# Layer 1: four narrow low-rank products side by side, their factors fetched by number, and a written TensorE order

## The chip, the cores and the metric

The kernel runs on one core of one Trainium2 chip. The metric is the device time of one execution in microseconds (us). The kernel before was run three times: the median is 3809.74 us, the lowest 3806.65 and the highest 3811.78. One more execution was recorded by the hardware profiler.

Five engines work side by side: TensorE (PE, matrix products, with its weight loads shown apart as PEld), VectorE (DVE), ScalarE (ACT), GpSimd (POOL) and SyncE (SP, which here issues DMA transfers). The matrix products write to PSUM. Everything is in fp32.

## The reference

The network has three layers and a tail. 64 sequences of 32 tokens, 2048 tokens of width 512, pass through all of it. The change touches only layer 1, and of it mainly the first half, a gated feed-forward block with low-rank updates. Each sequence has a number (`itok_B_2_6`, between 2 and 6), and by it picks its own pair A, B of rank 16 for each of the three products:

```python
def lora_add(base, inp, A, B):
    Ab = A[layer_idx][lora_indices]
    Bb = B[layer_idx][lora_indices]
    t = jnp.einsum('bri,bni->bnr', Ab, inp)
    return base + jnp.einsum('bor,bnr->bno', Bb, t) * SCALE
gate = lora_add(jnp.einsum('bnh,fh->bnf', x, W_gate), x, A_gate, B_gate)
up = lora_add(jnp.einsum('bnh,fh->bnf', x, W_up), x, A_up, B_up)
act = jax.nn.silu(gate) * up
down = lora_add(jnp.einsum('bnf,hf->bnh', act, W_down), act, A_down, B_down)
```

The width of `gate`, `up` and `act` is 1376. There are 16 sets of A and B. What the document calls the **first half** of an update is `t`, the product with A; the second half is the product with B.

The second part of layer 1 is a mixture of eight rank-16 updates on top of one base product: every token gets weights over the eight from a softmax and a threshold, and the result is added to x.

## The kernel before

A tile holds 128 tokens, that is four sequences. Layer 1 (`layer1`, L249 to L381) runs over eight groups g of G=2 tiles, so N=256 tokens and eight sequences. Every product has its contraction in chunks of at most 128: KC=4 chunks for the width 512, and the eleven chunks FC (`NFC`) for the width 1376, the last of which has 96.

A tile framework follows reads and writes, puts in the semaphores, and its scheduler chooses the order on each engine by what is ready; in layer 1 of this kernel nothing fixes the order on TensorE. Buffers come from pools: a second tile of the same tag waits until the first one's readers are done. In PSUM layer 1 has the tags `tr`, `low`, `gate` and `up`, two buffers each[...].

In one group:

- `inputs` (L282) loads two tiles of x through SP (`load`, L85) and gathers, with an indirect DMA on POOL (`gather`, L278), the rows of A and B of the eight sequences: eight times rank 16 gives 128 rows. There are six gathers: Ag, Au, Ad, Bg, Bu, Bd.
- x is transposed on TensorE and copied by ACT (`transposed`, L117 and L118) to xT.
- For Ag and Au the same is done, which gives AT; then one product of all 128 rows of A with all 256 tokens runs over four chunks (`accumulate`, L122, tile `pt`). Of the 128x256 results only those in which the row's sequence is the token's are wanted: DVE multiplies with the mask `own` (L311), which also holds the factor 0.5.
- Ad is transposed in eleven pieces (L317, tile `pa`) and copied by ACT to AdT.
- For each of the eleven chunks of features, `pg` and `pu` take four products with the weights and one with Bg or Bu each; ACT computes the sigmoid (L333), DVE multiplies twice (L334, L335) and writes actT.
- AdT with actT gives the first half of down, eleven products, masked at L339. `pz` is down's product, with Bd as its last step, copied by ACT to zT (L346).
- For each tile the mixture follows: `ph` (logits and the eight first halves, 137 columns), a chain of small operations on DVE and ACT, `hw` (L389), its transpose, `po` (base product and second halves), the sum with x (L381), and the store through SP (L382).

The inputs of group g+1 are asked for behind down of group g. Before layer 1, `layer0` computes in groups of four tiles and stores its results to memory (L245), from where layer 1 reads them; its last steps for a tile use POOL at L126, L242 and L243 and wait for a load of x (L85). Layer 0's first product `py` (L183) is already made of narrow products: 32 columns of weights, each for one sequence, four side by side, 512 moving columns. Layer 2 (attention) follows layer 1 and starts with loads of its weights and products at L504 and L509.

A record pair, a weight load and a matmul, is one pass; a product in fp32 takes two of them, a transpose takes one.

Of the kernel before, what the change touches and what calls it, by code (L numbers as in the profile page):

```python
# [24 lines left out]
F32 = mybir.dt.float32  # L25
# [35 lines left out]
class Common:  # L61


    def __init__(self, ctx, tc, a):
        self.tc, self.nc, self.a = tc, tc.nc, a
        self.last_load = None
        self.last_pe = None
        pool = ctx.enter_context(tc.tile_pool(name="common", bufs=1))
        self.ident = pool.tile([P, P], F32, name="ident")
        make_identity(self.nc, self.ident)  # L70
        self.minus_half = pool.tile([P, 2 * HK], F32, name="minus_half")
        self.nc.gpsimd.memset(self.minus_half, -0.5)
# [176 lines left out]


def layer1(c, kp, x_in, x_out):
    tc, nc, a = c.tc, c.nc, c.a
    G = 2
    N = G * P
    NE, R = 8, 16
    NFC = len(FC)
    with ExitStack() as ctx:
        aps = [ctx.enter_context(tc.tile_pool(name=f"l1_gathered{i}", bufs=1)) for i in range(2)]
        xp = ctx.enter_context(tc.tile_pool(name="l1_x", bufs=4))
        gup = ctx.enter_context(tc.tile_pool(name="l1_gate_up", bufs=1))  # L260
        wp = ctx.enter_context(tc.tile_pool(name="l1_weights", bufs=1))
        gp = ctx.enter_context(tc.tile_pool(name="l1_group", bufs=1))
        tp = ctx.enter_context(tc.tile_pool(name="l1_tile", bufs=2))
        ps = ctx.enter_context(tc.tile_pool(name="l1_psum", bufs=2, space=PSUM))


        ids = c.load(kp, "ids1", [P, NT // G], a["ids1"], I32)
# [8 lines left out]
        def gather(name, g):  # L276
            t = aps[g % 2].tile([P, a[name].shape[1]], F32, name=name)
            nc.gpsimd.indirect_dma_start(  # L278
                out=t, out_offset=None, in_=a[name],
                in_offset=bass.IndirectOffsetOnAxis(ap=rows[:, g:g + 1], axis=0))  # L280
            return t

        def inputs(g):
            xs = [c.load(xp, "xt", [P, D], x_in(G * g + t)) for t in range(G)]
            return xs, {n: gather(n, g) for n in ("Ag1", "Au1", "Ad1", "Bg1", "Bu1", "Bd1")}

        nxt = inputs(0)
        wg, wu = c.chunks(gup, "gate1T"), c.chunks(gup, "up1T")
        wd = wp.tile([P, NFC, D], F32, name="down1T")
        full = F1 // P  # L290
        nc.sync.dma_start(wd[:, :full, :], a["down1T"][:full * P].rearrange("(k p) n -> p k n", p=P))
        nc.sync.dma_start(wd[:F1 - full * P, full, :], a["down1T"][full * P:])
        wcat, wbase = c.chunks(wp, "cat1"), c.chunks(wp, "base1T")
        wB = c.load(wp, "B1", [P, D], a["B1"])
        bias = c.row(wp, "bias1")
        nb_thr = c.row(wp, "b_thr1")
        nc.vector.tensor_scalar(nb_thr, nb_thr, -1.0, None, ALU.mult)

        for g in range(NT // G):
            xs, sel = nxt  # L300
            xT = gp.tile([P, KC, N], F32, name="xT", bufs=2)
            for t in range(G):
                c.transposed(ps, "tr", xs[t], xT[:, :, t * P:(t + 1) * P])
            low = {}
            for n in ("Ag1", "Au1"):
                AT = tp.tile([P, KC, P], F32, name="AT")
                c.transposed(ps, "tr", sel[n], AT)
                pt = ps.tile([P, N], F32, tag="low", name="pt")
                c.accumulate(pt, [(AT[:, k, :], xT[:, k, :]) for k in range(KC)])
                low[n] = tp.tile([P, N], F32, name="low_" + n)  # L310
                nc.vector.tensor_tensor(low[n], pt, own, ALU.mult)  # L311
            AdT = gp.tile([P, NFC, P], F32, name="AdT")
            for i in range(0, NFC, KC):
                some = FC[i:i + KC]
                pt = ps.tile([P, KC, P], F32, tag="tr", name="pa")
                for m, (o, w) in enumerate(some):
                    nc.tensor.transpose(pt[:w, m, :], sel["Ad1"][:, o:o + w], c.ident)  # L317
                whole = sum(w == P for _, w in some)
                nc.scalar.copy(AdT[:, i:i + whole, :], pt[:, :whole, :])
                if whole < len(some):  # L320
                    w = some[-1][1]
                    nc.scalar.copy(AdT[:w, i + whole, :], pt[:w, whole, :])

            actT = gp.tile([P, NFC, N], F32, name="actT")
            for f, (o, w) in enumerate(FC):
                pg = ps.tile([P, N], F32, tag="gate", name="pg")
                c.accumulate(pg[:w], [(wg[:, k, o:o + w], xT[:, k, :]) for k in range(KC)]
                             + [(sel["Bg1"][:, o:o + w], low["Ag1"])])
                pu = ps.tile([P, N], F32, tag="up", name="pu")
                c.accumulate(pu[:w], [(wu[:, k, o:o + w], xT[:, k, :]) for k in range(KC)]  # L330
                             + [(sel["Bu1"][:, o:o + w], low["Au1"])])
                sg = tp.tile([P, N], F32, name="sg")
                nc.scalar.activation(sg[:w], pg[:w], AF.Sigmoid)  # L333
                nc.vector.tensor_tensor(sg[:w], sg[:w], pg[:w], ALU.mult)  # L334
                nc.vector.tensor_tensor(actT[:w, f, :], sg[:w], pu[:w], ALU.mult)  # L335
            pt = ps.tile([P, N], F32, tag="low", name="pt")
            c.accumulate(pt, [(AdT[:w, f, :], actT[:w, f, :]) for f, (_, w) in enumerate(FC)])
            low_d = tp.tile([P, N], F32, name="low_d")
            nc.vector.tensor_tensor(low_d, pt, own, ALU.mult)  # L339
            zT = gp.tile([P, KC, N], F32, name="zT")  # L340
            for m in range(KC):
                q = slice(m * P, (m + 1) * P)
                pz = ps.tile([P, N], F32, tag="gate", name="pz")
                c.accumulate(pz, [(wd[:w, f, q], actT[:w, f, :]) for f, (_, w) in enumerate(FC)]
                             + [(sel["Bd1"][:, q], low_d)])
                nc.scalar.copy(zT[:, m, :], pz)  # L346
            if g + 1 < NT // G:
                nxt = inputs(g + 1)

            for t in range(G):  # L350
                q = slice(t * P, (t + 1) * P)
                n_cat = NE * R + NE + 1
                ph = ps.tile([P, n_cat], F32, tag="up", name="ph")
                c.accumulate(ph, [(zT[:, k, q], wcat[:, k, :]) for k in range(KC)])
                h = tp.tile([P, n_cat], F32, name="h")
                nc.scalar.copy(h, ph)
                logits = h[:, NE * R:NE * R + NE]
# [16 lines left out]
                nc.vector.tensor_tensor(ws[:, 0:1], ws[:, 0:1], ws[:, 1:2], ALU.add)  # L374
                nc.vector.reciprocal(ws[:, 0:1], ws[:, 0:1])
                nc.vector.tensor_scalar(e, e, ws[:, 0:1], 2.0, ALU.mult, ALU.mult)
                po = ps.tile([P, D], F32, tag="low", name="po")
                mixture(c, tp, ps, po, h, e, lambda k: zT[:, k, q], wbase, wB)
                nc.gpsimd.tensor_tensor(xs[t], xs[t], bias, ALU.add)
                o = tp.tile([P, D], F32, name="o")  # L380
                nc.vector.tensor_tensor(o, po, xs[t], ALU.add)  # L381
                nc.sync.dma_start(x_out(G * g + t), o)  # L382


def mixture(c, pool, psum, out, h, weights, xT, wbase, wB):

    nc = c.nc
    hw = pool.tile([P, 8, 16], F32, name="hw")
    nc.vector.tensor_tensor(hw, h[:, :P].rearrange("p (e r) -> p e r", e=8),  # L389
                            weights.unsqueeze(2).to_broadcast([P, 8, 16]), ALU.mult)  # L390
    hwT = pool.tile([P, 1, P], F32, name="hwT")
    c.transposed(psum, "tr", hw.rearrange("p e r -> p (e r)"), hwT, 1)
    c.accumulate(out, [(xT(k), wbase[:, k, :]) for k in range(KC)] + [(hwT[:, 0, :], wB)])


def rotary_tables(c, pool, scratch):
# [707 lines left out]
def laid_out(i):  # L1104
# [5 lines left out]
    def low_rank(b):  # L1110
        return T(b, (0, 2, 1)).reshape(-1, b.shape[1])

    def per_row(ids, n):
        return T(np.repeat(ids, n).reshape(-1, P))
# [3 lines left out]
    lens = i["itok_B_207_1644"]  # L1118
    rank = 16
    k_cache = i["L2_cond_k_cache"].reshape(PAGES, PSIZE, HALVES, HKP, HD)  # L1120
    arrays = {
        "x": i["x"].reshape(B * S, D), "xT": T(i["x"].reshape(B * S, D)),

# [3 lines left out]
        "fc1T_0": T(i["L0_ffn_fc1_w"]), "fc2_0": i["L0_ffn_fc2_w"], "expert0": i["L0_ffn_expert_w"],  # L1127
        "gamma0": i["L0_ffn_ln_gamma"].reshape(1, D), "beta0": i["L0_ffn_ln_beta"].reshape(1, D),

        "ids1": per_row(i["itok_B_2_6"], rank),  # L1130
        "gate1T": T(i["L1_cond_W_gate"]), "up1T": T(i["L1_cond_W_up"]), "down1T": T(i["L1_cond_W_down"]),
        "Ag1": i["L1_cond_A_gate"][0].reshape(-1, D), "Bg1": low_rank(i["L1_cond_B_gate"][0]),
        "Au1": i["L1_cond_A_up"][0].reshape(-1, D), "Bu1": low_rank(i["L1_cond_B_up"][0]),
        "Ad1": i["L1_cond_A_down"][0].reshape(-1, F1), "Bd1": low_rank(i["L1_cond_B_down"][0]),
        "base1T": T(i["L1_ffn_W_base"]), "bias1": i["L1_ffn_b_base"].reshape(1, D),
        "cat1": np.concatenate([T(i["L1_ffn_A"].reshape(-1, D)), T(i["L1_ffn_W_gate"]),
                                T(i["L1_ffn_W_thr"])], axis=1),
# [45 lines left out]
```

## Time and profile before

| | |
|---|---|
| median of three runs | 3809.74 us |
| the profiled execution | 3798.88 us |
| its span, first to last instruction | 3797.0 us |
| mean granted TensorE clock in it | 0.997 |
| layer 1, steady: groups from 501.13, 592.34 and 683.53 us | 91.21, 91.19 and 91.17 us each |
| busy in the group from 592.34 us: PE, PEld | 90.69, 75.33 us |
| the same: DVE, ACT, POOL | 16.29, 14.27, 8.21 us |

In the tables of the profile a row names the line, the engine, the operation, and output<-input by the names of the tiles, then partitions x elements, and the count. After the bar come the busy time in us and the mean of one in ns, after a second bar the idle time of the engine just before, with what ended it. In a timeline a row begins with the start and the length in us. Matmuls are pipelined, so that the recorded length of one is longer than its distance to the next.

### The profile page before, as it was taken

Reading aid. Unit: us, or ns where it says so; the run is one execution under the profiler, and the core shown is the slowest. Engines: PE = TensorE matmul, PEld = TensorE weight load, DVE = VectorE, ACT = ScalarE, POOL = GpSimd, SP = SyncE. Lnnn points to the kernel's source line nnn. Section 1 sums busy time; section 2 is a strip of 40 time slices with the busy share of each in tenths; the row PEclk is TensorE's granted clock in tenths of the full one; section 3 lists DMA queues with packets and bytes.
Section 4 is the critical chain, followed back from the end, with each engine's and each line's share of the span. In section 5 each row is a group of like instructions: output and inputs, shape, how many; then the busy total and the mean of one; then the engine's idle time right before and its main releaser. Section 6 shows DMA issues by size and latency. Waiting matters only on the chain.

```text
span 3797.0 us, 60480 instructions
## 1 busy us (share of the span) xinstructions
PE 3732.0 (98%) x17992; PEld 2629.6 (69%) x17992; DVE 1797.3 (47%) x4863; ACT 1299.0 (34%) x3008; POOL 1284.4 (34%) x1289
## 2 busy tenths in 40 slices
PE   6999999999999999999999999999999999999999
PEld 2444788888886777777777777777777777777755
DVE  5443111111116566555655565556555665556433
ACT  0111111111114444444444444444444444444411
POOL 0112100000006454444444444444444554444222
PEclk9999999999999999999999999999999999999999
DMA  5104211111115433444334346454444444444522
GB/s 191 34 26 165 89 42 42 42 42 45 35 55 164 130 115 115 118 120 117 114 117 122 115 155 197 145 151 119 118 121 125 118 118 121 122 123 117 156 69 62
DMA packets 402036, 407.45 MB, mean 107 GB/s; under 512 B 48592, under 2 KB 312784, under 8 KB 401712
## 3 DMA queue, kind: packets, MB, share of 16 engines
q1 hardware_dynamic: 352560, 241.68, 20.9%
q0 software_dynamic: 46848, 157.72, 13.7%
q10 hardware_dynamic: 2304, 4.20, 0.3%
q8 instruction: 147, 2.41, 0.3%
q14 instruction: 177, 1.45, 0.1%
HBM read 382.44 MB, written 20.97 MB: 106 GB/s over the span
## 4 chain that ended last, share of the span: by engine, by line
PE 94%; DVE 1%; issue 1%; ACT 1%; SPq 1%; DVEq 1%; DMA 1%; POOL 1%; POOLq 0%; ACTq 0%
PE po L509 15%; PE sc L660 12%; PE py L509 12%; PE pq L509 11%; PE prT_ps L504 6%; PE pg L122 5%; PE pu L122 5%; PE pz L122 4%; PE po L958 3%; PE ph L122 3%; PE pv L509 3%; PE pk L509 3%; PE pd L228 2%; PE qkT_ps L504 2%; PE pt L122 2%; PE py L183 1%
## 5 line engine op out<-in xcount | busy, mean ns | idle before, releaser
L531 POOL DMA_INDIRECT vt<-in_v_rows,v_rows x512 | 499.4, 975 | 823.7 <-PE po L509 727.7
L509 PEld LDWEIGHTS po<-prT,vt 128*128 128x128 f32 x4096 | 530.5, 192 | 183.1 <-issue 177.5
L665 DVE CUSTOM_DVE_ANT_0 pr<-sc,mask 128x544 f32<-128x544 f32 x512 | 369.1, 721 | 434.5 <-PE sc L660 433.9
L660 PE MATMUL sc<-kt,qT 128*128 128x288 f32 (+1 forms) x2048 | 556.1, 394 | 7.3 <-DMA kt<-in_kT 4.1
L667 ACT ACTIVATE pr<-pr,low 128x544 f32<-128x544 f32 x512 | 383.2, 748 | 501.9 <-DVE low L665 499.8
L509 PE MATMUL po<-prT,vt 128*128 128x128 f32 x4096 | 541.7, 275 | 0.0
L660 PEld LDWEIGHTS sc<-kt,qT 128*128 128x128 f32 x2048 | 369.4, 191 | 183.9 <-issue 108.7
L509 PE MATMUL py<-wo,oT 128*128 128x512 f32 x1024 | 480.2, 592 | 0.8 <-DVE oT L701 0.8
L509 PE MATMUL pq<-wq,xT 128*128 128x512 f32 x1024 | 480.7, 593 | 0.0
L678 ACT COPY prT<-prT_ps 128x512 f32<-128x512 f32 x512 | 299.4, 585 | 417.5 <-PE prT_ps L504 413.3
L672 DVE TENSOR_SCALAR pr<-pr,low 128x512 f32<-128x512 f32 x512 | 312.6, 611 | 16.7
L504 PE MATMUL prT_ps<-ident,pr 128*128 128x128 f32 x2048 | 307.7, 273 | 0.3 <-DVE pr L672 0.3
L509 PEld LDWEIGHTS py<-wo,oT 128*128 128x128 f32 x1024 | 191.9, 190 | 137.9 <-issue 125.8
L509 PEld LDWEIGHTS pq<-wq,xT 128*128 128x128 f32 x1024 | 182.4, 190 | 130.1 <-issue 125.3
L669 DVE RECIPROCAL low<-low 128x1 f32<-128x1 f32 x512 | 83.1, 162 | 347.8 <-ACT pr L667 346.7
L504 PEld LDWEIGHTS prT_ps<-ident,pr 128*128 128x128 f32 x2048 | 241.4, 142 | 0.4 <-issue 0.4
L126 POOL TENSOR_TENSOR rs<-rs,minus_half 128x4 f32<-128x4 f32 x160 | 166.4, 1040 | 196.3 <-DVE rs L547 195.1
L563 POOL TENSOR_TENSOR rot<-rot,swapped 128x512 f32<-128x512 f32 x160 | 202.8, 1267 | 1.0
L670 ACT ACTIVATE own_pr<-pr,low 128x32 f32<-128x32 f32 x512 | 164.1, 321 | 113.4 <-DVE low L669 113.4
L546 DVE TENSOR_REDUCE rs<-squares 128x4 f32<-128x512 f32 x160 | 109.6, 685 | 168.4 <-ACT squares L544 164.4
L564 POOL TENSOR_TENSOR rot<-rot,rs 128x512 f32<-128x512 f32 x160 | 177.7, 1110 | 8.0
L122 PE MATMUL pg<-xT,gate1T 128*128 128x256 f32 (+1 forms) x704 | 170.2, 382 | 0.8 <-DVE sg L334 0.8
(217 smaller groups left out, 4815.4 us busy)
## 6 DMA issues: line engine op xcount, KB each, us to landing
kt<-in_kT SPq DMA_DIRECT2D x2048, 64.0 KB
xt<-x SPq DMA_DIRECT2D x48, 256.0 KB
wq<-in_WqT SPq DMA_DIRECT2D x12, 1024.0 KB
sets<-in_cond0T SPq DMA_DIRECT2D x4, 2048.0 KB
vt<-in_v_rows,v_rows POOLq DMA_INDIRECT x512, 3.7
wo<-in_WoT SPq DMA_DIRECT2D x8, 1024.0 KB
y<-y SPq DMA_DIRECT2D x32, 256.0 KB
xT<-in_xT SPq DMA_DIRECT2D x4, 1024.0 KB
```

The source lines that it names most:

```text
L122: self.nc.tensor.matmul(out, lhsT, rhs, start=i == 0, stop=i == len(pairs) - 1)
L126: self.nc.gpsimd.tensor_tensor(t, t, self.minus_half[:, :n], ALU.pow)
L504: c.on_pe(nc.tensor.transpose(pt[:, m, :], piece, c.ident))
L509: c.on_pe(nc.tensor.matmul(out, lhsT, rhs, start=first and i == 0, stop=last and i == len(pairs) - 1))
L531: nc.gpsimd.indirect_dma_start(out=vts[b % 2][:, n, :], out_offset=None, in_=a["v_rows"], in_offset=bass.IndirectOffsetOnAxis(ap=rows[h][: ...
L563: nc.gpsimd.tensor_tensor(r, r, tmp, ALU.add)
L564: last = nc.gpsimd.tensor_tensor(r, r, rs.unsqueeze(2).to_broadcast([P, REP, HD]), ALU.mult)
L660: c.on_pe(nc.tensor.matmul(sc[:, lo + n * PSIZE:lo + m * PSIZE].rearrange("p (n k) -> p n k", k=PSIZE), q, kt[:, n:m, g, :], start=True, s ...
L665: nc.vector.tensor_tensor_reduce(pr[:, :NK], sc[:, lo:lo + NK], masks[h, b], -SCALE, 3.0e38, ALU.add, ALU.min, low[:, 0:1])
L667: nc.scalar.activation(pr[:, :NK], pr[:, :NK], AF.Exp, bias=low[:, 0:1], scale=-1.0, accum_out=low[:, 1:2])
L672: nc.vector.tensor_scalar(pr[:, :L], pr[:, :L], low[:, 2:3], None, ALU.mult)
L678: nc.scalar.copy(prT, pt)
```

## The change

The first halves are computed in another way, and layer 1's loop is written anew around them.

- **Layout on the host.** The three A are laid out transposed and put together: `A1` has for each of the 16 sets 128 partitions with 304 numbers, 16 for each chunk of the contraction (4 of gate, 4 of up, 11 of down; down's width is filled with zeros to 11·128).
- **Fetch.** In place of the gathers of Ag, Au and Ad, SP reads the group's eight numbers into registers (`numbers`, which the kernel had before for another layer) and issues eight loads, each of one set (`load_by`). The three gathers of B stay on POOL. DVE copies the 16-wide pieces of eight sequences together (`firsts`).
- **Narrow products.** Two sequences at a time: 32 columns of weights (two sequences with 16 rows each) with the 64 tokens of those two. Four such products stand side by side, each with its own 32 partitions of the output. The mask (`masked`) picks the right half of each and spreads it to the full 128x256.
- **Order.** All of layer 1's products pass through `product`, which chains them by `on_pe` in the order of the program. The mixture of the group before stands between the features of the new group; x of the next group is transposed in this one; A and B of the next are asked for after feature 2, x after feature 4; the low product of the next group stands between the two parts of down.
- **PSUM.** The tags are `tr` (2 buffers), `acc` (4, each with gate and up of one chunk) and `lo` (2). zT is copied in two halves, one by ACT and one by DVE.

The core of the diff:

```diff
-            low = {}
-            for n in ("Ag1", "Au1"):
-                AT = tp.tile([P, KC, P], F32, name="AT")
-                c.transposed(ps, "tr", sel[n], AT)
-                pt = ps.tile([P, N], F32, tag="low", name="pt")
-                c.accumulate(pt, [(AT[:, k, :], xT[:, k, :]) for k in range(KC)])
-                low[n] = tp.tile([P, N], F32, name="low_" + n)
-                nc.vector.tensor_tensor(low[n], pt, own, ALU.mult)
...
+        def product(out, lhsT, rhs, start, stop):
+            c.on_pe(nc.tensor.matmul(out, lhsT, rhs, start=start, stop=stop))
...
+            def load_updates(self):
+                g = self.g
+                self.A = rp.tile([P, NS, a["A1"].shape[2]], F32, name="A")
+                numbers = c.numbers(a["ids1r"][0:1, NS * g:NS * (g + 1)], n_sets)
+                for j in range(NS):
+                    c.load_by(self.A[:, j, :], a["A1"][ds(numbers[j], 1)].rearrange("a p n -> (a p) n"))
+                self.B = {n: gather(n, g) for n in ("Bg1", "Bu1", "Bd1")}
+
+            def firsts(self, what):
+                lo, hi = (0, 2 * KC) if what == "x" else (2 * KC, 2 * KC + NFC)
+                t = gp.tile([P, hi - lo, NS, R], F32, name="first_" + what)
+                nc.vector.tensor_copy(t, self.A[:, :, lo * R:hi * R].rearrange("p j (k r) -> p k j r", r=R))
...
+            def low(self):
+                n = N // SEQ
+                pt = ps.tile([P, 2, n], F32, tag="tr", bufs=2, name="low_ps")
+                for u in range(2):
+                    for k in range(KC):
+                        for j in range(SEQ):
+                            q = slice(2 * R * j, 2 * R * (j + 1))
+                            product(pt[q, u, :], self.first_x[:, u * KC + k, q],
+                                    self.xT[:, k, j * n:(j + 1) * n], k == 0, k == KC - 1)
+                self.low_x = gp.tile([P, 2, N], F32, name="low_x", bufs=2)
+                self.masked(self.low_x, pt)
+
+            def low_down(self):
+                n = N // SEQ
+                pt = ps.tile([P, 1, n], F32, tag="lo", bufs=2, name="low_d_ps")
+                for f, (_, w) in enumerate(FC):
+                    for j in range(SEQ):
+                        q = slice(2 * R * j, 2 * R * (j + 1))
+                        product(pt[q, 0, :], self.first_d[:w, f, q],
+                                self.actT[:w, f, j * n:(j + 1) * n], f == 0, f == NFC - 1)
+                self.low_d = gp.tile([P, 1, N], F32, name="low_d")
+                self.masked(self.low_d, pt)
...
+        groups[0].x(0)
+        groups[0].x(1)
+        groups[0].firsts("x")
+        groups[0].low()
+        for g, new in enumerate(groups):
+            old = groups[g - 1] if g else None
+            then = groups[g + 1] if g + 1 < len(groups) else None
+            new.features(0)
+            if old:
+                old.choose(0)
+            new.features(1)
+            if old:
+                old.choose(1)
+            new.features(2)
+            new.firsts("down")
+            if then:
+                then.load_updates()
+            new.features(3)
+            if old:
+                old.turn(0)
+                old.base(0)
+                old.out(0)
+            new.features(4)
+            if old:
+                old.turn(1)
+                old.base(1)
+                old.out(1)
+            if then:
+                then.load_x()
+            for f in (5, 6, 7):
+                new.features(f)
+            if then:
+                then.x(0)
+            new.features(8)
+            if then:
+                then.x(1)
+            new.features(9)
+            if then:
+                then.firsts("x")
+            new.features(10)
+            new.down(range(NFC - 1), False)
+            new.low_down()
+            if then:
+                then.low()
+            new.down((NFC - 1,), True)
+        for f in (new.choose, new.base, new.turn, new.out):
+            for t in range(G):
+                f(t)
...
+    first = [i[f"L1_cond_A_{n}"][0] for n in ("gate", "up", "down")]
+    first = np.concatenate(first + [np.zeros((*first[0].shape[:2], -F1 % P), f32)], axis=2)
+    first_halves = T(first.reshape(*first.shape[:2], -1, P), (0, 3, 2, 1)).reshape(first.shape[0], P, -1)
```

`features` holds the products of one chunk for gate and up (ten products) with its sigmoid and its two multiplications, `down` the products of `pz`, `choose` the product `ph` and the small operations behind it, `base` the base product, `turn` the transpose of `hw`, and `out` the last product, the sum and the store. What they compute is as before.

## The prediction

> **What bounds the kernel now.** I first read the busy times and the chain of work that ended last.
>
> ```profile
> PE 3732.0 (98%) x17992; PEld 2629.6 (69%) x17992; DVE 1797.3 (47%) x4863; ACT 1299.0 (34%) x3008; POOL 1284.4 (34%) x1289
> PE 94%; DVE 1%; issue 1%; ACT 1%; SPq 1%; DVEq 1%; DMA 1%; POOL 1%; POOLq 0%; ACTq 0%
> ```
>
> TensorE (PE) is busy for 98% of the span and carries 94% of the chain. So layer 1 is priced in time of the matrix array: an edit counts by the array time it takes away or adds, plus what it does to the few waits.
>
> Next, one steady group of layer 1, 592.34 to 683.53 us (period 91.19). Its TensorE groups that the change removes are these, with the two slices of transposes:
>
> ```profile
> L122 PE MATMUL pt<-actT,AdT 128*128 128x256 f32 x20 | 4.5, 379 | 0.0
> L122 PE MATMUL pt<-xT,AT 128*128 128x256 f32 x16 | 3.6, 379 | 0.0
> L317 PE MATMUL pa<-ident,Ad 128*128 128x128 f32 x10 | 1.4, 275 | 0.0
> L117 PE MATMUL transposed<-ident,Au 128*128 128x128 f32 x4 | 0.7, 286 | 0.2 <-ACT xT L118 0.2
> L117 PE MATMUL transposed<-ident,Ag 128*128 128x128 f32 x4 | 0.6, 272 | 0.0
> L122 PE MATMUL pt<-actT,AdT 96*128 96x256 f32 x2 | 0.6, 379 | 0.0
> ```
>
> Matmuls overlap, so neither the mean of one nor the busy time is its price: the price is the distance from one start to the next. The timeline of TensorE gives it.
>
> ```profile
> 163.16 3.70 PE L122 MATMUL ph<-yT,up 128*128 128x512 f32 x8
> 166.79 1.93 PE L183 MATMUL py<-w,xT 128*32 128x512 f32 x16
> 168.64 1.12 PE L122 MATMUL ph<-yT,up 128*128 128x512 f32 x2
> ...
> 411.64 1.89 PE L122 MATMUL pg<-xT,gate1T 128*128 128x256 f32 x8
> 413.37 1.89 PE L122 MATMUL pu<-xT,up1T 128*128 128x256 f32 x8
> 417.45 3.72 PE L122 MATMUL pt<-xT,AT 128*128 128x256 f32 x16 [2.19 <-ACT AT L118]
> ...
> 592.34 0.60 PE L117 MATMUL transposed<-ident,xt 128*128 128x128 f32 x4
> 592.78 0.60 PE L117 MATMUL transposed<-ident,Ag 128*128 128x128 f32 x4
> 593.62 0.66 PE L117 MATMUL transposed<-ident,Au 128*128 128x128 f32 x4 [0.24 <-ACT xT L118]
> ```
>
> Eight records 256 wide take 413.37 − 411.64 = 1.73 us, 0.216 each; four 128 wide 0.44, 0.109 each; inside a run of 512-wide ones the single records start 0.429 apart. That is 0.834 ns a column plus some 2 ns. A full fp32 product is two records, a transpose one.
>
> **What goes.** Per group: pt<-xT,AT 16 × 0.216 = 3.45; pt<-actT,AdT 22 × 0.216 = 4.75; transposes of Ag and Au 8 and of Ad 11, 19 × 0.109 = 2.07. Sum 10.27 us, over eight groups **82.2 us**. All of it stands on the path: TensorE has no other work beside it. Their copies on ACT and the three indirect gathers on POOL (0.95 us each) go too; both engines were idle enough for that to be worth nothing here.
>
> **What comes: narrow products.** Per group 2·4·4 for gate and up and 11·4 for down, 76 products, each a 128x32 stationary tile and 64 moving columns: 152 pairs of weight load and matmul, 1216 in all. What a pair costs decides the case, and nothing so narrow runs before. The near row is layer 0's py: also 32 wide, also four side by side on the four column groups, 512 moving. In the timeline above 16 of its records take 1.85 us; one after another they would take 16 × 0.429 = 6.9. In the single records four matmuls start at 166.787, .794, .800 and .807, the next four at 167.240 to .260, then 167.669: four cost what one costs. Their weight loads also start 7 ns apart, and the second one of a column group 29 ns after its first, less than a 64-column stream needs. So a set of four with 64 columns: 64 × 0.834 + 2 = 56 ns, 14 ns a pair; 1216/4 × 0.056 = **17.0 us**.
>
> This stands only if instructions come fast enough: 8 in 56 ns. TensorE's queue shows semaphore events between its matmuls. Between two with nothing between there are 54 ns; with 8 instructions 74, with 28 instructions 114. That is about 2 to 2.5 ns an instruction, as in the py starts.
>
> A rule speaks against the change. The Trainium skill, "TensorEngine Tiling (Array Packing)", section Instruction Overhead, gives every matmul about 60 cycles and says "Don't take tiling factor from a dimension that's already small"; "TensorE: Matmul & The Clock Gate", section Back-to-back issue gap, has the same as a floor of about 25 ns up to 64 columns. The moving side shrinks here from 256 to 64 and the products multiply by four. By that rule the 1216 pairs cost 30.4 us, and the gain falls by 13. The py starts at 6.7 ns lie below 25, so I take the row; but py never needed such a rate for more than four pairs, so the rule's value stays in the range. The other bound: the closest lasting spacing that this trace shows, 109 ns (transposes), would make 1216 × 0.109 = 132.5 us.
>
> **Mode changes.** py between 128-wide runs costs 1.85 − 4 × 0.429 = 0.13 us, and the ph run after py 3.63 − 8 × 0.429 = 0.20: 0.33 a round trip. The change has 9 narrow blocks (a first low, seven times low_down with the next low, a last low_down): **3.0 us**.
>
> **Stalls in the steady group.** Dense, the records of a group are worth 90.02 us; the period is 91.19, so 1.15 us is lost: before Au 0.84 − 0.44 = 0.40, before the transpose of hw 0.43, the rest in small pieces. In the new order x is transposed during features 7 to 9 of the group before, and choose, turn, base and out of the old group stand between features, each a block of 4.3 us. So those waits go. What is late next: Bd needs low_d, which DVE masks (some 0.43 us by its 256-column row) while low (0.9 us) and one product (0.43) run; the first Bg needs low_x (512 columns, 0.7) while down's last chunk (3.5) runs. Cover lost there would cost at most 0.5 a group. Gain 7 × 1.0, less 1 for what I miss: **+6** (range 0 to 8).
>
> DVE gets copies of A's columns, 1024 and 1408 elements a partition; by L179's copy of 512 at 0.42 us that is 0.84 and 1.15 us, on an engine busy 16.3 of 91 us. Behind them wait a feature's two multiplications; the four accumulators give three blocks, 13 us, of slack. ACT goes between sigmoid and exp twice per group instead of once: two table loads of 1.28 us more, under the same slack. SP gets eight loads of A per group and their number reads; it issued two loads and two stores in 91 us, and an issue by number with its register work takes 0.4 to 0.5 us (row of kt's loads). The next x loads and the stores of o stand behind them, 20 us and more before they are needed. A has two buffers, so its 1.2 MB a group, as much as the gathers moved, comes a group ahead. All of these: nothing.
>
> **Edges.** These waits stand before and at the start of layer 1:
>
> ```profile
> PE ph L122 <- DVE z L241: 4.2, 2, 2.3
> PE transposed L117 <- issue: 2.8, 1, 2.8
> PE pt L122 <- ACT AT L118: 2.2, 1, 2.2
> PE transposed L117 <- ACT xT L118: 1.4, 1, 1.4
> PE pg L122 <- DVE sg L334: 0.8, 1, 0.8
> ```
>
> The first is layer 0's: at 324 and 332 us z comes late because POOL issues layer 1's twelve gathers between its own steps and because a load of x waits. Now six gathers stand there, but SP gets 16 loads of A and slow number reads in front of layer 0's stores and loads of x. Taken +1 (range −4 to +4.2). The 2.2 goes with AT, but the fixed order can no longer run gate products ahead of the low products while x or A is late: +2 (range −4 to +3). The end of the last group keeps its serial chain (1127.8 to 1139.7), and attention's own order is unchanged: nothing.
>
> **Sum.** 82.2 − 17.0 − 3.0 + 6 + 2 + 1 = 71.2 us. The profiled execution took 3798.88 with a span of 3797.0; so the span should be 3725.8 and that execution's like 3727.7. The median of the three runs, 3809.74, lies 10.9 above the profiled one; that offset stays: **3738 us**.
>
> **Rivals.**
> - *Pairs cost more than the row says, but pay* (25 to 72 ns). For: no narrow pair has run at a lasting rate in this trace. Against: the queue's 2 ns an instruction. At 55 ns: 66.9 us instead of 17.0, gain 21, 3788. With 25 ns, 3752, it is still my forecast's range.
> - *Narrow products end slower than before*. One mechanism, in the narrow blocks: pairs that don't overlap, at 109 ns as the transposes. 88.2 (all but the pairs) − 132.5 = −44: 3854. It decides from 88.2/1216 = 72.5 ns a pair. Against: py overlaps.
> - *The fixed order turns a hidden wait into one per group*: TensorE can take no other product while low waits for first_x, or Bd for low_d, or features for an accumulator behind a table load. 1 to 4 us a group: 3752 to 3776. Against: the slack counted above.
> - *The removed time returns at the edges* (SP's loads of A against layer 0's loads of x): both lower bounds at once, −8 instead of +3: 3749.
>
> Chances: forecast 0.70, dearer pairs 0.11, slower 0.06, a new wait per group 0.09, edges 0.04. **Range 3720 to 3780**: the lower end has the stalls and edges at their best (10 us) and 8 for the run, the upper one a pair of 25 ns with a wait of 3 us per group. A difference of 0.2% (7.6 us) is about what this measurement tells from none. Pairs from 66 to 79 ns would lie within it: same 0.03; slower 0.07; faster 0.90.
>
> **What would show it.** The period between groups: 91.2 before, 82.5 by these terms (90.02 − 10.27 = 79.75 dense, 2.13 narrow, 0.33 mode change, 0.3 lost). Starts of low_ps and low_d_ps in sets of four 56 ns apart; a narrow block of 152 pairs 2.1 us long, 3.8 by the rule, 16.6 if pairs don't overlap. No waits for hw or for xT. At 318 to 335 us, the waits for z; at 402 to 425 us, low waiting for first_x. I am wrong if the block is longer than 4 us, or if a wait of over 0.5 us returns in every group.

## The result

The changed kernel takes 3738.94 us (median of four runs, 3737.36 to 3742.54) against 3810.76 us before (four runs, 3806.65 to 3812.89). The ratio is 0.9816 with a 95% interval of 0.9801 to 0.9831: 71.8 us or 1.8% faster. The forecast was 3738.

The page of the changed kernel answers to the two lines shown of the kernel before: busy times, and the chain that ended last by engine.

```profile
PE 3668.9 (98%) x18752; PEld 2575.0 (69%) x18752; DVE 1813.8 (48%) x4879; ACT 1281.3 (34%) x2950; POOL 1261.0 (34%) x1265
PE 95%; SPq 1%; DMA 1%; issue 1%; DVEq 1%; DVE 1%; ACT 0%; POOL 0%; ACTq 0%; POOLq 0%
```

TensorE has 760 records more and is busy 63 us less, and it is still the bound. Where the time went is seen by cutting both traces at the same events (first product, first transpose of x in layer 1, first one in layer 2):

| us | before | after |
|---|---|---|
| start to first product | 23.60 | 27.55 |
| layer 0 | 378.61 | 380.52 |
| layer 1 | 738.39 | 667.77 |
| layer 2 and tail | 2656.43 | 2664.70 |
| span | 3797.0 | 3740.5 |

Layer 1 gave 70.6 us. The first and the last row are the same instructions in both kernels. Over all thirteen traces of this study they scatter from 23.6 to 27.8 and from 2656.4 to 2666.3, and the kernel before's trace has the lowest of both: its profiled execution was a lucky one. So the two spans differ by only 56.5 us where the medians differ by 71.8.

The steady groups of layer 1, in windows of one group (length; then busy time and records of PE, PEld, DVE, ACT, POOL; clock; DMA share; GB/s):

```profile
531.83:614.07 82.24, 82.24 (x515) 68.19 (x514) 18.84 (x53) 13.12 (x28) 5.37 (x5) 1.00 0.16 49
861.35:944.80 83.45, 82.31 (x516) 68.21 (x515) 18.84 (x53) 13.12 (x28) 5.38 (x5) 1.00 0.10 33
```

91.19 us became 82.24, but one group takes 1.2 more with the same work. The timeline of TensorE around the narrow block of these two groups:

```profile
563.02 1.44 PE L292 MATMUL low_d_ps<-actT,first_down 128*32 128x64 f32 x88
564.28 1.08 PE L292 MATMUL low_ps<-xT,first_x 128*32 128x64 f32 x64
565.28 0.70 PE L292 MATMUL pz<-actT,down1T 96*128 96x256 f32 x2
...
892.53 1.44 PE L292 MATMUL low_d_ps<-actT,first_down 128*32 128x64 f32 x88
893.79 1.08 PE L292 MATMUL low_ps<-xT,first_x 128*32 128x64 f32 x64
896.01 0.70 PE L292 MATMUL pz<-actT,down1T 96*128 96x256 f32 x2 [1.14 <-issue]
```

152 pairs from 563.02 to 565.28 are 2.26 us. In the single records fours start 56 ns apart, 14.0 ns a pair. In the other group 1.14 us stand empty behind the block, with "issue" as the reason: no wait that the profile knows of. The group before it has such a gap of 0.56 us just behind its block, the one after it one of 0.5 us in its block; by the lengths of the groups it is 2.3 us in all. Experiment 5 looks for the cause.

The waits of TensorE from 300 to 480 us:

```profile
PE ph L122 <- DVE z L241: 3.9, 2, 3.8
PE xT_ps L327 <- issue: 2.8, 1, 2.8
PE low_ps L292 <- ACT xT L328: 1.7, 1, 1.7
PE pd L232 <- ACT eT L118: 0.5, 1, 0.5
```

The waits for AT and sg are gone; z in layer 0 is as late as before (3.9 against 4.2), for another reason (experiment 7).

### The profile page after: what moved, and what is told of

Read it like the earlier page. It is cut to its first block, busy times and chain, and to the rows that moved or that the text cites. A ratio compares the mean times of both kernels' runs of the same rounds, so it can differ in the third digit from the quotient of the medians.

```text
span 3740.5 us, 62127 instructions
## 1 busy us (share of the span) xinstructions
PE 3668.9 (98%) x18752; PEld 2575.0 (69%) x18752; DVE 1813.8 (48%) x4879; ACT 1281.3 (34%) x2950; POOL 1261.0 (34%) x1265
## 4 chain that ended last, share of the span: by engine, by line
PE 95%; SPq 1%; DMA 1%; issue 1%; DVEq 1%; DVE 1%; ACT 0%; POOL 0%; ACTq 0%; POOLq 0%
PE po L621 15%; PE sc L772 12%; PE pq L621 12%; PE py L621 11%; PE gate_up L292 10%; PE prT_ps L616 6%; PE pz L292 4%; PE po L1070 3%; PE pv L621 3%; PE pk L621 3%; PE ph L122 3%; PE pd L228 2%; PE po L292 2%; PE qkT_ps L616 2%; PE py L183 2%
## 5 line engine op out<-in xcount | busy, mean ns | idle before, releaser
L784 DVE TENSOR_SCALAR pr<-pr,low 128x512 f32<-128x512 f32 x512 | 325.4, 635 | 16.6
L376 DVE TENSOR_TENSOR sg<-sg,gate_up 128x256 f32<-128x256 f32 (+1 forms) x88 | 37.0, 420 | 278.3 <-ACT sg L375 278.3
```

Source lines behind the costliest of these rows:

```text
L784: nc.vector.tensor_scalar(pr[:, :L], pr[:, :L], low[:, 2:3], None, ALU.mult)
```

## The experiments

Ratios are to the kernel before on the same chip. Where two experiments are compared, the length of layer 1 in the trace (cut as above) is used, since it leaves out the scatter of the rest.

**1. Full-width products (wide).** Is it the width that pays, or the order and the fetch?

```diff
-                        for j in range(SEQ):
-                            q = slice(2 * R * j, 2 * R * (j + 1))
-                            product(pt[q, u, :], self.first_x[:, u * KC + k, q],
-                                    self.xT[:, k, j * n:(j + 1) * n], k == 0, k == KC - 1)
+                        product(pt[:, u, :], self.first_x[:, u * KC + k, :],
+                                self.xT[:, k, :], u == 0 and k == 0, u == 1 and k == KC - 1)
```

with the same in `low_down`, and the mask taken in full width.

> The changed kernel with its first halves as full products again: 128 columns of A with all 256 tokens, 19 products a group in place of 76 narrow ones, everything else (A fetched by number, the order) kept. My theory (a product costs array time, narrow pairs overlap): per group 38 records x 0.216 = 8.2 us come and 2.13 + 0.2 to 0.33 go, so +5.8 us a group and +46 us in all: about 3785. If the gain came mostly from the order and the fetch and the narrow products only about break even: within 10 us of 3739.

Measured: 3780.85 us, ratio 0.9927 (0.9911 to 0.9944). The window of one group:

```profile
449.55:537.54 87.99, 87.99 (x402) 73.28 (x401) 18.94 (x53) 13.13 (x28) 5.45 (x5) 1.00 0.15 46
```

87.99 − 82.24 = 5.75 us a group, as computed. Layer 1 is 43.1 us longer; the sum of 46 is not reached mainly because the changed kernel loses those 2.3 us to pauses and this one, with fewer instructions, has none. The second theory is out: the narrow products carry more than half of the gain.

**2. A gathered and transposed again (gathered).** Narrow products and order stay.

```diff
-                for j in range(NS):
-                    c.load_by(self.A[:, j, :], a["A1"][ds(numbers[j], 1)].rearrange("a p n -> (a p) n"))
+                self.A = {n: gather(n, g) for n in ("Ag1", "Au1", "Ad1")}
...
+                        c.on_pe(nc.tensor.transpose(pt[:w, m, :], self.A[n][:, o:o + w], c.ident))
```

> The changed kernel with A gathered by rows on POOL and transposed on TensorE again, narrow products and order kept. My theory: 19 transposes a group come back at 0.109 us each, 2.07 us a group, +16.6 us in all and up to 5 us more if a transpose waits for a copy: 3755 to 3761. If SP's loads of A cost time at the edges of layer 1, part of it is given back there: 3750.

Measured: 3752.13 us, ratio 0.9848 (0.9831 to 0.9864). A group takes 84.77 us, 2.53 more (2.07 for the transposes and 0.46 beside them); layer 1 takes 685.07, 17.3 more (20.2 for eight groups, less the changed kernel's 2.3 of pauses, of which this kernel's trace has none; the remaining 0.6 was not traced). The median rose by only 13 because layer 0 was 2.8 us shorter without SP's loads of A (377.73 against 380.52) and the rest scattered. Both theories hold, each for its part.

**3. The narrow products alone (before_narrow).** The kernel before, its two `accumulate` calls with A replaced:

```diff
+            for i, (lhsT, rhs) in enumerate(pairs):
+                for j in range(SEQ):
+                    q = slice(2 * R * j, 2 * R * (j + 1))
+                    nc.tensor.matmul(pt[q, :], lhsT[:, q], rhs[:, j * n:(j + 1) * n],
+                                     start=i == 0, stop=i == len(pairs) - 1)
```

> The kernel before with only its products with A made narrow (gathers, transposes and the order as before). My theory: per group 8.2 us go, 2.13 come and two narrow blocks with two mode changes (0.2 to 0.33 each) come: 5.4 to 5.7 us a group, 43 to 46 us: 3765 to 3768. If narrow blocks amid an order chosen by readiness are torn apart or wait for copies of the transposed A, less than 35 us are gained: over 3775.

Measured: 3780.55 us, ratio 0.9918 (0.9902 to 0.9935). Only 30 us: my theory missed by a third. Its narrow blocks, in TensorE's timeline, with POOL's rows of the same time below:

```profile
590.40 0.86 PE L292 MATMUL pt<-xT,AT 128*32 128x64 f32 x44
591.50 0.32 PE L292 MATMUL pt<-xT,AT 128*32 128x64 f32 x5 [0.23 <-issue]
592.22 0.33 PE L292 MATMUL pt<-xT,AT 128*32 128x64 f32 x5 [0.40 <-issue]
592.94 0.38 PE L292 MATMUL pt<-xT,AT 128*32 128x64 f32 x10 [0.39 <-issue]
...
590.21 0.97 POOL L278 DMA_INDIRECT Ag<-in_Ag,rows  x1
591.48 0.95 POOL L278 DMA_INDIRECT Au<-in_Au,rows  x1 [0.31 <-issue]
```

44 pairs run at full rate, then five at a time, 0.72 us apart. The block takes 2.8 us in place of 1.03, low_down's 2.3 in place of 1.37. No wait is named, and nothing in the scheduler's order tore the block apart. In the last groups, where no further gather is issued, the very same instructions run without a pause. That made the gathers the suspect.

**4. The gathers taken away (no_gathers).** before_narrow, with groups 2 to 7 reusing the rows of groups 0 and 1:

```diff
-            return xs, {n: gather(n, g) for n in ("Ag1", "Au1", "Ad1", "Bg1", "Bu1", "Bd1")}
+            if g < 2:
+                kept[g] = {n: gather(n, g) for n in ("Ag1", "Au1", "Ad1", "Bg1", "Bu1", "Bd1")}
+            return xs, kept[g % 2]
```

> before_narrow with the gathers of groups 2 to 7 left out (they reuse the rows of groups 0 and 1, so the updates of those groups are computed with other sequences' A and B; the products are as many). If the pauses inside the narrow blocks come from gathers running beside them: all 16 blocks take 1.03 and 1.37 us, 16 us less than before_narrow, a ratio to the kernel before of 0.987 to 0.988. If the pauses belong to the blocks themselves: ratio as before_narrow's, 0.992.

Measured: ratio 0.9879 (0.9864 to 0.9894), 3763.45 us. All blocks behind the first one are undisturbed (1.03 and 1.37 us each; the first, at 420 us, 1.07), and layer 1 falls from 709.04 to 692.91. So gathers beside narrow blocks cost 16.1 us there, and narrow products without them gain 738.39 − 692.91 = 45.5, within my 43 to 46. The full-width products of the kernel before lose nothing to gathers: its last group, behind the last gather (945.84 us), takes 91.21 us like the others.

Does the same happen in the changed kernel? Its gathers of Bg and Bu come at feature 10, 17 us ahead of its narrow block. Two runs bring them together: one moves low there, one moves feature 10.

```diff
 (low_early)
             new.features(10)
+            if then:
+                then.low()
             new.down(range(NFC - 1), False)
             new.low_down()
-            if then:
-                then.low()
```

> The changed kernel with the next group's low moved from behind low_down to right behind feature 10, where POOL issues the gathers of Bg and Bu. Seven mode changes more, 0.2 to 0.33 us each: +1.4 to +2.3 us, 3741. If an indirect gather on POOL slows the supply of TensorE's instructions (in before_narrow every narrow block beside a gather pauses for 0.6 us after each 5 pairs, and the four without one beside them don't): the block of 64 pairs takes 2 to 2.7 us in place of 0.9 in the groups that still gather, and +7 to +13 us: 3746 to 3752.

```diff
 (beside_gather)
-            new.features(10)
             new.down(range(NFC - 1), False)
-            new.low_down()
+            new.features(10)
             if then:
                 then.low()
+            new.low_down()
```

> The changed kernel with feature 10 moved behind down's first ten chunks, and low and low_down right behind it, so that a block of 152 pairs starts as POOL issues the gather of Bu. low_down then waits for feature 10's sigmoid and products: 0.5 to 1.2 us a group, +4 to +10 us on the changed kernel. If a gather beside a narrow block slows TensorE's instructions: also pauses of 0.6 us after each 5 pairs inside the block, 0.6 to 1.3 us in each of the six groups that still gather, and none in the last two. In low_early a block of 64 pairs at the same place showed none: if that holds, no pauses beyond the wait for feature 10.

low_early measured 3736.63 us, ratio 0.9825 (0.9808 to 0.9841): no pause in any block behind the first, 1.03 us each, although the gather of Bu was issued 0.34 us into them (543.30, the block at 542.96). A group takes 82.75 us, 0.51 more than the changed kernel's. 0.33 of it is a mode change (switching from wide to narrow products and back); the rest stands in front of Bd, because low's 0.9 us no longer cover the mask of low_d. beside_gather measured 3746.18, ratio 0.9834 (0.9819 to 0.9849). Its block beside the same gather:

```profile
559.62 1.26 PE L292 MATMUL low_ps<-xT,first_x 128*32 128x64 f32 x52
561.32 0.38 PE L292 MATMUL low_ps<-xT,first_x 128*32 128x64 f32 x10 [0.43 <-issue]
```

A pause of 0.63 us between two starts, in each of the six groups that still gather, and none of that kind in the last two. So the effect is not the older kernel's alone; a gather is needed for it. It isn't enough: low_early's block of 64 pairs at the same distance from the same gather ran through. Its end is no explanation: in beside_gather the pairs first halt 0.31 us after the start of Bu's gather (559.97), and low_early's block went on to 0.54 us after it. What decides between these two is open.

**5. Long narrow blocks (narrow3).** Every narrow block three times:

```diff
-                for u in range(2):
+                for u in (0, 1) * 3:
...
-                for f, (_, w) in enumerate(FC):
+                for f, (_, w) in [*enumerate(FC)] * 3:
```

> The changed kernel with every narrow block's products done three times over (each pass starts its sums anew, so the result stays): 2432 pairs more, no mode change more. If a pair costs its quarter of a stream however long the block is: 2432 x 0.014 = +34 us, 3773, blocks of 456 pairs 6.4 us long. If the instructions of TensorE, fetched in pages of 256 (16 KB), set the rate in a long block (two of the changed kernel's eight blocks stood 1.1 and 0.3 us with no wait near such a fetch): a page per 2.3 us is 128 pairs, 18 ns a pair and pauses of about 0.5 us at each page: +44 to +50 us, 3785.

Measured: 3803.21 us, ratio 1.0002 (0.9993 to 1.0010); layer 1 takes 66.4 us more. More than both theories said, on the side of the second. TensorE's timeline of one block:

```profile
574.63 3.66 PE L292 MATMUL low_d_ps<-actT,first_down 128*32 128x64 f32 x244
579.38 0.48 PE L292 MATMUL low_d_ps<-actT,first_down 128*32 128x64 f32 x18 [1.09 <-issue]
...
582.83 1.42 PE L292 MATMUL low_ps<-xT,first_x 128*32 128x64 f32 x84 [1.46 <-issue]
```

Between the pauses the pairs run at 14 ns. Counted over all records of TensorE's queue (loads, matmuls and semaphore events), the pauses stand at numbers 4032, 4288, 4544, then 5824, 6080, 7360 and so on: always 192 above a multiple of 256. The trace also has the packets that carry instructions (queue q8, 16 KB each): 172 of them here against 153 in the changed kernel, for 4864 more records on TensorE, which is 256 a packet. I call one packet's instructions a page. From one pause's end to the next there are 3.45 us (579.38 to 582.83) to 4.3, in which 256 instructions, 128 pairs, go through: 27 ns a pair at best. The packet itself takes about 1 us, and the first instruction behind a pause starts 2.3 to 3.0 us after its packet (577.04 and 579.38, for one). I had taken 2.3 us a page from the one pause in the changed kernel, which is the time from the fetch's start to the first instruction behind it and not the time between two pages.

The three pauses of the changed kernel stand at numbers 7872, 8896 and 9920, 192 above a multiple of 256 as well, and in its second trace (after_again, below) all three are there again, with 1.1, 1.7 and 0.3 us. A block has 304 instructions, so a second page end can fall into it or right behind it, sooner after the first than a fetch takes. In the groups before, the second end comes later, among wide products that use an instruction in 108 ns. Two more runs fit. low_early has blocks of 128 and 176 instructions and none of these pauses, so its layer 1 is only 0.3 us longer (668.05 against 667.77) though each group is 0.51 longer. onebyone (below) has blocks of 304 but uses an instruction in 21 ns, and has none either. Why gathered, with the same blocks at other places in the pages, has none was not worked out.

**6. One column group after the other (onebyone).** The same products, loops exchanged:

```diff
-                    for k in range(KC):
-                        for j in range(SEQ):
+                    for j in range(SEQ):
+                        for k in range(KC):
```

> The changed kernel with the same narrow products in another order: all of one column group (8 or 22 records) before the next group's, so that neighbours are on the same 32 columns. If side by side depends on the order of issue: a pair costs its stream of 56 ns, 1216 x 0.042 = +51 us: 3790. Rival: TensorE sends each column group's instructions to its own queue and looks past the waiting ones, since py's starts (first passes of four products before their second passes) already stand in another order than the program's: then the block stays near 14 to 30 ns a pair, +0 to +20 us: 3739 to 3759.

Measured: 3767.94 us, ratio 0.9889 (0.9872 to 0.9905); layer 1 takes 698.60, 30.8 more, between the two theories. The timeline of one block:

```profile
566.22 4.35 PE L292 MATMUL low_d_ps<-actT,first_down 128*32 128x64 f32 x85
570.36 0.24 PE L292 MATMUL low_ps<-xT,first_x 128*32 128x64 f32 x1
570.40 0.22 PE L292 MATMUL low_d_ps<-actT,first_down 128*32 128x64 f32 x1
```

6.48 us in place of 2.26. Inside one column group starts are 56 ns apart, the full stream. But a new column group begins 1.035 us after the one before, where 22 records of 56 ns would be 1.23: its first three or four records run beside the last ones of the old group, as the mixed rows of low_ps and low_d_ps show. TensorE does look past a waiting instruction, but only by a few pairs. Being side by side must be in the order of issue.

**7. The second group's A out of layer 0 (late_A1).** SP's rows in the changed kernel's second trace, where layer 0's stores and loads of x should follow:

```profile
299.88 0.38 SPq L85 DMA_DIRECT2D xt<-in_x  x1
300.53 15.95 SPq L98 DMA_DIRECT2D A<-in_A  x16
318.33 0.33 SPq L245 DMA_DIRECT2D x<-z  x1
318.94 0.34 SPq L85 DMA_DIRECT2D xt<-in_x  x1
```

The edit makes B1's load the one behind which the next number reads are placed:

```diff
-        wB = c.load(wp, "B1", [P, D], a["B1"])
+        wB = wp.tile([P, D], F32, name="B1")
+        c.load_by(wB, a["B1"])
```

> The changed kernel with the loads of A for group 1 issued on SP behind layer 1's weights, so that eight loads of A in place of 16 stand between layer 0's stores and loads of x. If those 16 loads (16.3 us on SP) are what made z late at 329.7 us in the changed kernel's trace (3.8 us of waiting): 2 to 4 us less, 3735 to 3737. If the wait is POOL's gathers and the load of x itself, as in the kernel before: within 1 us of 3739.

Measured: 3729.41 us, ratio 0.9804 (0.9787 to 0.9820), on a chip whose kernel before took 3804.34. To compare it with the changed kernel on one chip, both ran again:

> The changed kernel itself, unedited, on the same chip as late_A1_again, for the comparison of the two: ratio to the kernel before 0.9816 as it was.

> The edit of late_A1 again, beside the changed kernel on one chip. If the 16 loads of A in layer 0 cost what the two traces say (first product to layer 1: 380.5 us with them, 376.5 without eight of them): 3 to 4 us below after_again. If that was the scatter of single executions: within 1 us of it.

after_again: 3739.71 us (3736.12 to 3741.32, five runs), ratio 0.9818 (0.9804 to 0.9831). late_A1_again: 3735.00 (3732.31 to 3736.47, five runs), ratio 0.9804 (0.9791 to 0.9818). 4.7 us less, somewhat more than the 3 to 4 expected, with almost separate runs, although the two intervals of the ratios overlap. SP spends 4.15 us in place of 15.95 on A there, and TensorE's waits from 300 to 430 us change as follows, after_again first and then late_A1_again:

```profile
PE ph L122 <- DVE z L241: 5.5, 2, 3.0
```

```profile
PE ph L122 <- DVE z L241: 1.9, 1, 1.9
```

Layer 0 takes 376.5 and 376.1 us in the two traces with the edit, 380.5 and 381.4 in the changed kernel's two, and 378.7 to 381.5 in the five other variants that keep the 16 loads there (wide, onebyone, narrow3, low_early, beside_gather). By its medians this is the fastest version of the study.

## Why the prediction was right

The median difference is 71.8 us, the sum said 71.2. Term by term, from layer 1's length in the traces, the change taken apart in three steps: narrow products (before to no_gathers), order (no_gathers to gathered), fetch (gathered to after).

| step | predicted | measured |
|---|---|---|
| products narrow | 8 × 8.2 − 17.0 − 3.0 = 45.6 | 738.39 − 692.91 = 45.5 |
| order: stalls, start of layer 1 | 6 + 2 | 692.91 − 685.07 = 7.8 |
| 19 transposes a group | 16.6 | 685.07 − 667.77 = 17.3 |

The middle step has the gathers of groups 2 to 7 back on its second side, away from the blocks, and it also holds the new PSUM tags and the split copy of zT, so it is not a pure one; no run tests the order alone.

That the first row agrees to 0.1 us is chance in part. no_gathers has 16 narrow blocks and not nine, so its own sum is 65.6 − 17.0 − 16 × 0.33 = 43.3. Its steady groups give that: 85.75 us each, 5.46 less than before, 43.7 for eight. Of the other 1.8 us, 1.5 is a shorter wait for AT at the start of the layer (0.7 against 2.2). The seven mode changes that the joined blocks save, 2.3 us, then belong to the second row, where 10.3 stand against 7.8. The three rows together, 70.2 against 70.6, don't depend on this split.

- **A pair at 14 ns.** Right: 14.0. Reading py's single starts as sets of four, scaled from 512 to 64 columns, was the step that decided the case. The rule of about 25 ns a matmul, which the prediction put at 13 us, doesn't bind here: neighbours on different column groups start 7 ns apart and sets of four 56. On one column group 64 columns take 56 ns anyway.
- **Instructions fast enough.** Half right. The queue's 2 to 2.5 ns hold for what is at hand. But I read them from stretches of up to 28 instructions, and a block has 304. Page ends cost 2.3 us in the changed kernel's trace, which no term held, and with three times the products the blocks 66 us more in place of 34.
- **Mode changes.** Right: the first narrow start is 0.309 us behind the last 256-wide one, where 0.216 is normal; the first wide start behind the block comes 0.135 us late and the second 0.105. Together 0.33 a block, as the py rows gave it.
- **Steady stalls.** Better than the 0.3 a group left for them: 79.75 + 2.13 + 0.33 = 82.21 of 82.24. Bd's cover was thin: with low moved away it cost some 0.18 a group (low_early).
- **Edges.** Layer 0 was put at −1 us and came at +1.9 in the first trace: the gathers that left POOL were paid back by SP, as the bound of −4 had it, and late_A1 shows the price of half of the 16 loads, 4.7 us in the medians. The +2 at layer 1's start can't be told apart from the rest of the second row.
- **The profiled execution** was forecast at 3727.7 us and took 3742.5. I carried the 10.9 us between the one profiled run and the median of before over as if they belonged to the method; they belonged to that run. The forecast of the median stands on the difference, so it was not touched.
- **Luck.** The mechanism held, but a miss of only 0.6 us is better than its terms: the pauses (2.3) and layer 0 (2.9 less than forecast) were not in the sum, layer 0 alone scatters by 3 us between traces with the same instructions in it, and the two profiled spans differ by 56.5 where the medians differ by 71.8.

The rivals: lastingly dearer pairs came only where a run provoked them (narrow3, onebyone) and beside gathers; one wait per group did not come; the edges took about 2 us.

## What to carry over

Small products on different column groups cost a quarter of their stream each if neighbours in the order of issue lie on different column groups; put the loop over column groups innermost. Keep such blocks well below a page of 256 instructions (those of 128 and 176 showed no pause at page ends), and away from indirect gathers: at 7 ns an instruction the supply of instructions is the next bound. Put loads whose data are ready early where no queue of later stores and loads stands behind them: eight of them in the wrong place gave back some 4.7 us of 72. And take differences between medians, not between two single profiled executions.

## What the runs showed of the hardware

- TensorE's instructions come in pages of 256 (19 more packets for 4864 more instructions), and in a long block of narrow pairs a page lasts at least 3.45 us: 13.5 ns an instruction, while those at hand are taken at 7 ns. The pauses stand at page ends in narrow3, in both traces of the changed kernel and in both with late_A1's edit.
- An indirect gather on POOL (0.95 us of issue) can stop TensorE's narrow block with no wait that the profile names: for 0.6 us, after every five pairs of a stretch in before_narrow, once per group in beside_gather, and in no_gathers in no block behind the first. Through what the two meet was not found out, and low_early's blocks, which were not touched, are not explained.
- In onebyone three to four pairs of the next column group ran ahead beside the waiting ones of the old.
